# Four-layer graph network, one core: the third pass over the adjacency by half rows on four column groups

## The chip, the cores and the metric

The kernel runs on one core of one Trainium2 chip. The metric is the device time of one execution in microseconds (us), as a median of several runs. The engines are TensorE (PE), VectorE (DVE), ScalarE (ACT), GpSimd (POOL) and SyncE (SP), whose queue here issues most loads; ACT and POOL can issue DMAs too.

## The reference

`x` is 2708 x 128, `adj` a sparse 2708 x 2708 matrix with weights. Four layers follow each other, each as `x = layernorm(x + layer(x, adj))`:

```python
# layer 0: z = leaky(lap(A) x W1 + b1); S = exp(-dist(z) / 2), the 4 nearest of each row kept
out = _lap_mul(S + A, x) @ W2 + b2            # _lap_mul(A, x) = d * (A @ (d * x)), d = rowsum(A) ** -0.5
# layer 1
den = exp(leaky_relu(s_row[:, None] + s_col[None, :], 0.01))
num = A @ den
H   = A @ ((den / num) @ XW)                  # den / num where num != 0
# layer 2: h = (dinv * A * dinv) @ x; h @ W.T + b
# layer 3: relu([x, A @ x] @ W.T + b)
```

Layer 1 is the one that the change touches: `num` is a dense 2708 x 2708 product of `adj` with a matrix whose entries depend on a sum of a row number and a column number only.

## The kernel before, in words

**Tiling.** The rows of `adj` (its transpose `adjT` is streamed from HBM) are 22 row tiles: 21 full ones of 128 rows and a last one of 20 (`FULL = 21`). The 2708 columns are six chunks (four of 512, one of 384, one of 276), or two halves of 1354 (`HALF`). Row tiles 16 to 21 stay resident (`res`); tiles 0 to 15 (`S = 16`) are streamed again in each pass over `adj`.

**Order of the whole.** Pass one (degrees and A x, L428), the search for nearest neighbours (L699 to L702, bound by DVE), pass two (`by_panels`, L189, with a queue `due` of small steps that have due times), then the third pass (L1316 to L1396), then a block loop for layer 1 (`block_layer`, from L1556, 44 steps), then layers 2 and 3 with passes of their own.

**How layer 1 avoids the dense product.** Rows and columns are sorted by rank, and the sorted `num` is computed in 22 x 2 blocks (`NQ = 22` groups of columns, two halves). Within a block the change from one row to the next is a short list of rows of `adj`: `slot_i` lists them, POOL gathers them from HBM into `ring` (L1449, two gathers a step), `lw` holds their weights. A chain of four blocks (`CH = 4`, 11 chains, `NCH`) hands its last row on through `carry` (SP: L1586 writes, L1455 reads back). The chains' first rows come from the third pass.

**The third pass.** It computes 22 sums, `A` times a 128 x 22 weight matrix per row tile (`lc`, 32 columns wide, 22 used), and puts them into `carry`. By column chunk `c` the 20 row tiles 0 to 19 go in groups of four to the four groups of 32 columns of PE, so four different row tiles add up side by side in one bank (`part_sum`, matmul L1322). Tile 20 and the last 20 rows of three chunks go to these groups together. So at the end four partial sums per chunk have to be folded: `end_sums(c)` copies the bank on ACT (L1331), multiplies by the 0/1 matrix `sel` on PE (L1333) and copies into `carry` on ACT (L1334). It is called behind the first panel of chunk c + 1, for the last chunk behind everything. `fold` and `sel` are built in the neighbour search by six DVE operations.

A streamed panel is 4 row tiles by one chunk (1 MB, rows of 2,048 bytes). Six slots hold such panels: four in `ring` and two in `more`, all filled ahead of the pass (L178 is the load).

**Work in between.** `between(c, i0)` (L1338) puts the sorting work on PE, DVE and ACT between the panels, in an order written out by hand: `last_xw`, `find_blocks`, `into_places` (L1169, tiles `js` and `sl`), `count` (L1255, L1262), `ranked` (POOL: memset of `xws` L1193 and then `SOON` = 14 fetches of X W rows, L1039), `listed` (L1279, gives `slot_i`), and six groups of `weights` (transposes L1058 on PE, then ACT L1308 for groups 1 and 3, DVE L1312 to L1314 for the others).

**Into the block loop.** A flag read from the chip chooses the branch (L1464). Then ACT loads a table (L1561), the first num (L1571) waits for gathers, the rows out of `carry` and the weights; Ln (L1403), Exp (L1406), err (DVE L1413), L1417, L1420 follow, then hacc (PE L1428). Each of the first eight steps also carries one of the remaining fetches (L1039) on POOL.

Of the kernel before, what the change touches and what calls it, by code (L numbers as in the profile page):

```python
# [8 lines left out]
F32 = mybir.dt.float32  # L9
# [7 lines left out]
P = 128  # L17
CW = 512
# [3 lines left out]
KC = 126  # L22
CH = 4
MAGIC = 1.5 * 2**23
OOB = 4095
# [5 lines left out]
class Due:  # L31
# [5 lines left out]
    def at(self, n, f, *args):  # L37
        self.work.append((n, len(self.work), f, args))
        self.work.sort(key=lambda w: w[:2])
# [13 lines left out]
def kernel(  # L53
# [16 lines left out]
    nc = tc.nc  # L70
# [7 lines left out]
    C = len(starts)  # L78
# [17 lines left out]
    def few(c):  # L96
        g = c % GROUPS * 32
        return slice(g, g + LAST)
# [12 lines left out]
    def acc_tile():  # L111
        return acc_pool.tile([P, CW], F32, tag="acc", name="acc")

    def mis_tile():
        return mis_pool.tile([P, CW], F32, tag="mis", name="mis")
# [55 lines left out]
    def load_panel(g, c, pool=None):  # L171

        if pool is None:
            s = slots[taken[0] % len(slots)]
            taken[0] += 1
        else:
            s = pool.tile([P, 4, CW], F32, tag="strip", name="part")
        nc.sync.dma_start(  # L178
            s[:, :, : cw[c]],
            adjT[g * 4 * P : (g + 1) * 4 * P, cols[c]].rearrange("(t p) k -> p t k", p=P),  # L180
        )
        return s
# [587 lines left out]
    rows_h = atile([1], "rows_h")  # L770
    spare = near.rearrange("p t k -> p (t k)")
    few_n, rk_f, neg_r = (spare[:, n * T : (n + 1) * T] for n in range(3))
    fold, sel = spare[:, 3 * T : 3 * T + 2 * NCH], spare[:, 3 * T + 2 * NCH : 3 * T + 2 * NCH + 2 * NB]
    nc.vector.memset(rk_f, float(OOB))
    nc.vector.tensor_add(fold, ident[:, : 2 * NCH], ident[:, 32 : 32 + 2 * NCH])
    for g in (64, 96):
        nc.vector.tensor_add(fold, fold, ident[:, g : g + 2 * NCH])
    nc.vector.memset(sel, 0.0)
    nc.vector.tensor_copy(
        sel.rearrange("p (a v) -> p a v", v=2 * CH)[:, :, :2], fold.rearrange("p (a v) -> p a v", v=2)  # L780
    )
    nc.vector.memset(rows_d, 0.0)
    add_bias(b2_sb)
    rk = rk_pool.tile([P, T], F32, tag="rk", name="rk")
# [182 lines left out]
    near_at = [24 + (23 * t) // 5 for t in range(T)]  # L967
    for t in range(T):
        at(near_at[t], sum_near, t)

    ended = [-16]
    behind_last = []
# [48 lines left out]
        due.flush()  # L1021
    late.close()
    more = ExitStack()
    more_pool = more.enter_context(tc.tile_pool(name="more", bufs=2, side="right"))
    slots += [more_pool.tile([P, 4, CW], F32, tag="more", name="more") for _ in range(2)]
    taken[0] = 0
    G = S // 4
    panels = [(c, g) for c in range(C) for g in range(G)]
    ready = [load_panel(g, c) for c, g in panels[: len(slots)]]
    sums.close()  # L1030
    lwx = ctx.enter_context(tc.tile_pool(name="lwx", bufs=1))
    val_q = lwx.tile([P, T, 3, NQ], F32, tag="xws", name="val_q")
    val_b = lwx.tile([P, T, 3, NB], F32, tag="lw", name="val_b")
    plain = lwx.tile([P, 2], F32, tag="plain", name="plain")

    SOON = 14

    def fetch_xw(xws, q):
        nc.gpsimd.indirect_dma_start(  # L1039
# [5 lines left out]
    with tc.tile_pool(name="rank", bufs=1) as rank:  # L1045
# [38 lines left out]
        def to_all(c_part):  # L1084
            n = c_part.shape[-1]
            out = mis_tile()
            nc.tensor.matmul(out[:, :n], lhsT=ones_f, rhs=c_part, start=True, stop=True)
            return out
# [27 lines left out]
        def last_xw():  # L1116

            for t in last_ts:
                p = pw[t]
                pt = mis_tile()  # L1120
                nc.tensor.transpose(pt[:, :p], xs[:p, t, :], ident[:p, :p])
                xT = small.tile([P, P], F32, tag="z", name="xT")
                nc.scalar.copy(xT[:, :p], pt[:, :p])
                po = mis_tile()
                nc.tensor.matmul(po[:p, :D], lhsT=xT[:, :p], rhs=wa_sb, start=True, stop=True)
                row = small.tile([P, P], F32, tag="junk", name="row")
                nc.scalar.copy(row[:p], po[:p, :D])
                nc.gpsimd.dma_start(xw_rows[t * P : t * P + p, :], row[:p])
# [185 lines left out]
            nc.vector.tensor_scalar_max(w, w, 0.0)  # L1314

        carry = big.tile([P, NQ * P], F32, tag="y", name="carry")  # L1316
        sums_of, begun = {}, set()

        def part_sum(c, i, g, src, rows=slice(None), last=False):
            if c not in sums_of:  # L1320
                sums_of[c] = acc_tile()
            nc.tensor.matmul(  # L1322
                sums_of[c][32 * g : 32 * g + 32, : cw[c]], lhsT=lc[rows, i, :], rhs=src,
                start=(c, g) not in begun, stop=last,
            )
            begun.add((c, g))

        def end_sums(c):
            w = cw[c]
            tot = rank.tile([P, CW], F32, tag="tot", name="tot")  # L1330
            nc.scalar.copy(tot[:, :w], sums_of[c][:, :w])  # L1331
            ps = mis_tile()
            nc.tensor.matmul(ps[: 2 * NB, :w], lhsT=sel, rhs=tot[:, :w], start=True, stop=True)  # L1333
            nc.scalar.copy(carry[: 2 * NB, cols[c]], ps[: 2 * NB, :w])  # L1334

        work = {}

        def between(c, i0):  # L1338

            if (c, i0) == (0, 4):  # L1340
                last_xw()
            if (c, i0) == (0, 8):
                c_edge = to_all(c_part)
                find_blocks(c_edge)
                work["js"] = js_pool.tile([P, CW], F32, tag="places", name="js")
            if (c, i0) == (1, 4):
                for n in range(3):
                    into_places(work["js"], hot[n], val_q[:, :, :2, :], n)
                hot.append(ones_at(b_j, 3))
                find_values()  # L1350
            if (c, i0) == (2, 0):
                work["counts"] = count()
            if (c, i0) == (2, 4):
                into_places(work["js"], hot[3], val_q[:, :, :2, :], 3)
                find_places(*work["counts"])
                work["xws"] = ranked(work["js"])
                hot[:] = [ones_at(pos, n, spot) for n in range(3)]
            if (c, i0) == (3, 0):
                work["sl"] = js_pool.tile([P, CW], F32, tag="places", name="sl")
                for n in range(3):  # L1360
                    into_places(work["sl"], hot[n], val_b, n)
                hot.append(ones_at(pos, 3, spot))
            if (c, i0) == (3, 4):
                into_places(work["sl"], hot[3], val_b, 3)
                work["lw"] = listed(work["sl"])
            if (c, i0) in ((3, 8), (3, 12), (3, 16), (4, 0), (4, 4), (4, 8)):
                weights(work["lw"], 4 * work["groups"])
                work["groups"] += 1

        work["groups"] = 0  # L1370
        nc.vector.tensor_reduce(lone_part, lone, AX.X, ALU.add)
        for c in range(C):
            w = cw[c]
            begins = c % GROUPS == 0
            for i0 in range(0, FULL - 1, 4):
                if i0 < S:
                    n = c * G + i0 // 4
                    part = ready[n] if n < len(ready) else load_panel(i0 // 4, c)
                for i in range(i0, i0 + 4):
                    src = part[:, i % 4, :w] if i < S else res[:, i - S, cols[c]]  # L1380
                    part_sum(c, i, i % 4, src, last=i0 + 4 >= FULL - 1 and (i % 4 > 0 or not begins))
                if i0 == 0 and c:
                    end_sums(c - 1)
                if i0 + 4 >= FULL - 1 and begins:
                    for n in range(c, c + GROUPS):
                        part_sum(n, FULL - 1, n - c, res[:, FULL - 1 - S, cols[n]])
                    for n in range(c, c + GROUPS):
                        part_sum(n, FULL, 0, res[few(n), FULL - S, cols[n]], few(n), last=n == c)
                    if c == 0:
                        ps = mis_tile()  # L1390
                        nc.tensor.matmul(ps[:, :1], lhsT=ones_f, rhs=lone_part, start=True, stop=True)
                        nc.scalar.copy(lone_all, ps[:, :1])
                between(c, i0)
        xws, lw = work["xws"], work["lw"]
        end_sums(C - 1)
        order.close()  # L1396
    del slots[SLOTS:]
    more.close()

    def invert(w, num, pool, bufs, sums=True):  # L1400
# [44 lines left out]
    def load(i):  # L1445
        h, q = steps[i]
        rows[i] = strip(i).rearrange("p (n k) -> p n k", n=2)
        for n in range(2):
            nc.gpsimd.indirect_dma_start(  # L1449
                out=rows[i][:KC, n, :], out_offset=None, in_=adj_half[:, :],  # L1450
                in_offset=bass.IndirectOffsetOnAxis(ap=slot_i[h][:KC, 2 * q + n : 2 * q + n + 1], axis=0),
                bounds_check=2 * N - 1, oob_is_err=False,
            )
            b = block(2 * q + n)
            nc.sync.dma_start(  # L1455
                rows[i][KC : KC + 2, n, :], carry[2 * b : 2 * b + 2, h * HALF : (h + 1) * HALF]
            )

    m_rows = row_tile("m_rows").rearrange("p (t d) -> p t d", d=D)
    mT = m_rows.rearrange("p t d -> p (t d)")[:, :N]  # L1460
# [306 lines left out]
```

## Time and profile before

| | us |
|---|---|
| three runs | 1094.03, 1094.39, 1097.14 |
| median | 1094.39 |
| profiled execution | 1093.01 |
| its span | 1091.3 |
| PE busy (share of the span) | 1000.2 (92%) |
| DVE busy | 638.5 (59%) |
| ACT busy | 336.6 (31%) |
| POOL busy | 265.2 (24%) |
| mean granted PE clock | 0.965 |
| third pass, first add (L1322) | 459.82 |
| last add of the third pass | 524.48 |
| first num of the block loop (L1571) | 530.06 |
| first Ln (L1403) | 533.92 |

How to read it: a line of the timeline gives start, duration, engine, source line, operation, result `<-` operands with partitions x elements, how many records, and in brackets the idle time before it and what ended that. PE records of a float matmul are several to a matmul, so `x8` can be four matmuls; matmuls on different column groups of PE overlap. "SPq" is SP's queue, "remote" a releaser that the trace doesn't name.

### The profile page before, as it was taken

The numbers are of one execution on the slowest core, as the hardware profiler recorded it, in microseconds if no ns is written. First come the engines' busy times: TensorE is split into PE (matmuls) and PEld (weight loads), VectorE is DVE, ScalarE is ACT, GpSimd is POOL, SyncE is SP. The second block draws the span as 40 slices with busy tenths as digits, with TensorE's granted clock in tenths as the row PEclk, the third lists the DMA queues.
The fourth block names the chain that finished last, engine by engine and source line by source line (L and its number), as shares of the span: only waits on it lengthen the run. The fifth ranks groups of instructions, "written<-read, shape, count | busy, mean of one in ns | idle before, by whom it ended". The sixth has DMA issues, their size and how long they took to land.

```text
span 1091.3 us, 11487 instructions
## 1 busy us (share of the span) xinstructions
PE 1000.2 (92%) x3697; PEld 482.7 (44%) x3697; DVE 638.5 (59%) x1363; ACT 336.6 (31%) x617; POOL 265.2 (24%) x339
## 2 busy tenths in 40 slices
PE   0898999999987898798799999999999999999996
PEld 0445544444433455543233333334444644565444
DVE  5885448999934477772499999998112112132122
ACT  0000126555401144612467776665001100011000
POOL 4000000000575463015584344430112100000000
PEclk9889999999997899798899999999999999999998
DMA  9999340000383556497545545555775865574752
GB/s 341 357 329 276 102 137 1 0 1 1 100 279 89 186 160 205 141 369 228 136 131 153 154 122 166 143 143 181 230 232 157 275 229 183 170 238 158 240 158 77
DMA packets 109380, 190.31 MB, mean 174 GB/s; under 512 B 13666, under 2 KB 46706, under 8 KB 109310
## 3 DMA queue, kind: packets, MB, share of 16 engines
q1 hardware_dynamic: 91408, 151.79, 42.7%
q0 software_dynamic: 17728, 37.62, 12.5%
q8 instruction: 31, 0.51, 0.2%
q14 instruction: 39, 0.32, 0.1%
q10 hardware_dynamic: 174, 0.08, 0.0%
HBM read 214.37 MB, written 4.16 MB: 200 GB/s over the span
## 4 chain that ended last, share of the span: by engine, by line
PE 66%; DVE 16%; DMA 6%; issue 4%; ACT 3%; another core or an unknown queue 2%; POOL 2%; SPq 1%; POOLq 0%; DVEq 0%; ACTq 0%
PE acc L204 31%; PE num L1571 9%; PE hacc L1428 9%; PE acc L428 7%; DVE where L702 6%; DVE near L701 5%; DMA res<-in_adjT 3%; PE acc L1322 2%; PE mis L285 1%; PE acc L699 1%; DMA part<-in_adjT 1%; DMA got<-y_rows,where 1%; ACT junk L911 1%; DVE both L483 1%
## 5 line engine op out<-in xcount | busy, mean ns | idle before, releaser
L1449 POOL DMA_INDIRECT ring<-in_adjT,slot_i x88 | 95.4, 1084 | 117.7 <-PE num L1571 88.8
L1571 PE MATMUL num<-ring,lw 128*64 128x512 f32 (+1 forms) x528 | 115.6, 560 | 3.3 <-DVE err L1413 1.4
L1428 PE MATMUL hacc<-inv,xws 128*128 128x512 f32 (+1 forms) x264 | 111.7, 559 | 0.6 <-issue 0.3
L699 PE MATMUL acc<-zT,z 128*128 128x512 f32 (+2 forms) x252 | 102.2, 552 | 0.0
L1403 ACT ACTIVATE inv<-num,plain 128x1024 f32<-128x1024 f32 x88 | 80.6, 916 | 60.9 <-PE num L1571 38.6
L253 POOL TENSOR_TENSOR rstd<-rstd,minus_half 128x4 f32<-128x4 f32 (+1 forms) x18 | 17.3, 961 | 313.4 <-DVE rstd L252 313.4
L234 ACT COPY gb<-acc 128x512 f32<-128x512 f32 (+2 forms) x18 | 9.6, 535 | 251.1 <-PE acc L204 251.1
L1413 DVE TENSOR_TENSOR err<-inv,num 128x1024 f32<-128x1024 f32 x88 | 74.4, 854 | 20.4 <-ACT inv L1406 17.6
L700 ACT COPY key<-acc 128x512 f32<-128x512 f32 (+2 forms) x126 | 67.1, 535 | 55.1 <-issue 27.9
L204 PE MATMUL acc<-ring,y 128*128 128x512 f32 (+2 forms) x192 | 81.8, 556 | 0.5 <-issue 0.5
L1428 PEld LDWEIGHTS hacc<-inv,xws 128*128 128x128 f32 x264 | 46.5, 189 | 77.6 <-issue 45.2
L729 POOL DMA_INDIRECT got<-y_rows,where x66 | 70.2, 1063 | 37.5 <-DVE near_sum L742 18.9
L204 PE MATMUL acc<-ring,xs 128*128 128x512 f32 (+2 forms) x192 | 77.9, 549 | 0.0
L1420 DVE SCALAR_TENSOR_TENSOR inv<-gb,g_inv,inv 128x1024 f32<-128x1024 f32 x88 | 77.0, 913 | 0.1
L204 PE MATMUL acc<-ring,carry 128*128 128x512 f32 (+2 forms) x192 | 74.5, 542 | 0.0
L204 PE MATMUL acc<-ring,m_rows 128*128 128x512 f32 (+2 forms) x192 | 74.3, 542 | 0.0
L1417 DVE SCALAR_TENSOR_TENSOR inv<-err,inv 128x1024 f32<-128x1024 f32 x88 | 72.4, 861 | 0.1
L1406 ACT ACTIVATE inv<-inv 128x1024 f32<-128x1024 f32 x88 | 67.6, 768 | 2.8
L699 PEld LDWEIGHTS acc<-zT,z 128*128 128x128 f32 x252 | 45.8, 190 | 50.4 <-issue 45.0
L575 POOL TENSOR_TENSOR slot_e<-near,sim 128x44 f32<-128x44 f32 (+2 forms) x3 | 0.7, 245 | 269.7 <-DVE d2inv L603 267.6
L1571 PEld LDWEIGHTS num<-ring,lw 128*64 128x64 f32 x528 | 36.2, 138 | 65.0 <-issue 46.7
L701 DVE MAX8 near<-key 128x8 f32<-128x2708 f32 x21 | 62.2, 2964 | 2.7 <-ACT key L700 2.7
(378 smaller groups left out, 1392.0 us busy)
## 6 DMA issues: line engine op xcount, KB each, us to landing
ring<-in_adjT SPq DMA_DIRECT2D x86, 1024.0 KB
ring<-in_adjT SPq DMA_DIRECT2D x19, 768.0 KB
part<-in_adjT SPq DMA_DIRECT2D x12, 1024.0 KB
ring<-in_adjT SPq DMA_DIRECT2D x19, 552.0 KB
res<-in_adjT SPq DMA_DIRECT2D x4, 1280.0 KB
more<-in_adjT SPq DMA_DIRECT2D x4, 1024.0 KB
part<-in_adjT SPq DMA_DIRECT2D x3, 768.0 KB
part<-in_adjT SPq DMA_DIRECT2D x3, 552.0 KB
```

The source lines that it names most:

```text
L204: nc.tensor.matmul(accs[c][: lhsT.shape[-1], :w], lhsT=lhsT, rhs=src, start=start, stop=stop)
L428: nc.tensor.matmul(accs[c][:, : cw[c]], lhsT=y[:, i, :], rhs=src[:, : cw[c]], start=first, stop=last)
L699: nc.tensor.matmul(pks[c][:p, : cw[c]], lhsT=z2[:, :p], rhs=zT[:, cs], start=False, stop=True)
L701: nc.vector.max(near[:p, t, :], key[:p])
L729: nc.gpsimd.indirect_dma_start(out=got[:p, :], out_offset=None, in_=y2_rows[:, :], in_offset=bass.IndirectOffsetOnAxis(ap=where[:p, t, k : ...
L1403: nc.scalar.activation(inv, num[:, :w], AF.Ln, scale=plain[:, 0:1], bias=plain[:, 1:2])
L1413: nc.vector.tensor_mul(err, inv, num[:, :w])
L1417: nc.vector.scalar_tensor_tensor(inv, err, 2.0, inv, op0=ALU.subtract, op1=ALU.mult)
L1420: nc.vector.scalar_tensor_tensor(inv, gb[:, col : col + w], g_inv[:, q : q + 1], inv, op0=ALU.max, op1=ALU.mult)
L1428: nc.tensor.matmul(haccs[:, o:e], lhsT=xws[:, q, :], rhs=inv[:, o:e], start=(q == 0), stop=(q == NQ - 1))
L1449: nc.gpsimd.indirect_dma_start(out=rows[i][:KC, n, :], out_offset=None, in_=adj_half[:, :], in_offset=bass.IndirectOffsetOnAxis(ap=slot_i[ ...
L1571: nc.tensor.matmul(num[n * (BJ + 2) : (n + 1) * (BJ + 2), o:e], lhsT=lw[:, 2 * q + n, :], rhs=rows[i][:, n, c0 + o : c0 + e], start=True, ...
```

## The change

- The third pass goes by *lines*: one row tile by half of the columns (128 x 1354, 693 KB, rows of 5,416 bytes). The four column groups of PE take four quarters (339, 339, 338, 338 columns) of one row tile, all with the same weights, so the bank holds finished sums and nothing is folded. Order: first half, then second half, 16 lines each.
- Nine *berths* hold lines: six half strips of `ring` and three in `more`, filled ahead of the pass. Load n + 9 is issued behind line n. Lines from 27 on use only the three in `more`.
- The resident tiles' halves (`own_line`) and the last 20 rows (`add_last_rows`) stand between the lines. For the latter the last rows are loaded again by quarters into other partition groups (8 small SP loads), and put back after the pass (6).
- At the end of each half two ACT copies take the bank to `heads`, and four DMAs on ACT's queue put its rows into `carry`, partitions 96 to 117; `load` takes a chain's first rows from there.
- The order by hand is the list `turns`. `fold`, `sel` and their six DVE operations go; the memset of `rk_f` moves into pass two.
- `SOON` is 6: six fetches of X W rows ahead of the loop, sixteen in its steps.

The core of the diff:

```diff
-    for g in (64, 96):
-        nc.vector.tensor_add(fold, fold, ident[:, g : g + 2 * NCH])
...
+    at(20, nc.vector.memset, rk_f, float(OOB))
...
+    berths = [ring[:, n * HALF : (n + 1) * HALF] for n in range(2 * STRIPS)]
+    berths += [more_pool.tile([P, HALF], F32, tag="more", name="more") for _ in range(3)]
+    AHEAD = len(berths)
+    lines = [(i, h) for h in range(2) for i in range(S)]
+    def line_at(n):
+        return berths[n % AHEAD if n < 3 * AHEAD else AHEAD - 3 + n % 3]
+    def load_line(n):
+        i, h = lines[n]
+        nc.sync.dma_start(line_at(n), adjT[i * P : (i + 1) * P, h * HALF : (h + 1) * HALF])
...
-    SOON = 14
+    SOON = 6
...
-            nc.scalar.copy(tot[:, :w], sums_of[c][:, :w])
-            ps = mis_tile()
-            nc.tensor.matmul(ps[: 2 * NB, :w], lhsT=sel, rhs=tot[:, :w], start=True, stop=True)
-            nc.scalar.copy(carry[: 2 * NB, cols[c]], ps[: 2 * NB, :w])
...
+        for g in range(4):
+            for h in range(2):
+                n0, n1 = h * HALF + edges[g], h * HALF + edges[g + 1]
+                nc.sync.dma_start(res[few(g), FULL - S, n0:n1], adjT[FULL * P :, n0:n1])
+        def add_line(i, h, src, last=False):
+            for g in range(4):
+                nc.tensor.matmul(
+                    banks[h][32 * g : 32 * g + 32, : edges[g + 1] - edges[g]], lhsT=lc[:, i, :],
+                    rhs=src[:, edges[g] : edges[g + 1]], start=(h, g) not in begun, stop=last,
+                )
+                begun.add((h, g))
+        def add_last_rows(h):
+            for g in range(4):
+                n0, n1 = h * HALF + edges[g], h * HALF + edges[g + 1]
+                nc.tensor.matmul(
+                    banks[h][32 * g : 32 * g + 32, : n1 - n0], lhsT=lc[few(g), FULL, :],
+                    rhs=res[few(g), FULL - S, n0:n1], start=False, stop=False,
+                )
+        def end_half(h):
+            tot = heads[:, h * span : (h + 1) * span]
+            nc.scalar.copy(tot[:, : edges[4] - edges[3]], banks[h][:, : edges[4] - edges[3]])
+            nc.scalar.copy(tot[:64, edges[4] - edges[3] :], banks[h][:64, edges[4] - edges[3] : span])
+            for g in range(4):
+                w = edges[g + 1] - edges[g]
+                nc.scalar.dma_start(
+                    carry[HEADS : HEADS + 2 * NCH, h * HALF + edges[g] : h * HALF + edges[g + 1]],
+                    tot[32 * g : 32 * g + 2 * NCH, :w],
+                )
...
+        def line(n):
+            for _ in range(n):
+                at = loaded[0]
+                loaded[0] += 1
+                i, h = lines[at]
+                add_line(i, h, line_at(at), last=at == 2 * S - 1)
+                if at + AHEAD < 2 * S:
+                    load_line(at + AHEAD)
...
+        turns = [
+            (line, 4), (blocks_of_edges,), (line, 5), (own_line, 2), (last_xw,), (in_rank_order, 0), (line, 2),
+            (in_rank_order, 1), (line, 2), (in_rank_order, 2), (count_lone,), (line, 2), (counts,), (line, 1),
+            (add_last_rows, 0), (own_line, 3), (line, 2), (ranks_known,), (line, 2), (own_line, 1), (in_list_order, 0),
+            (line, 2), (in_list_order, 1), (in_list_order, 2), (line, 2), (own_line, 1), (in_list_order, 3), (line, 1),
+            (next_weights,), (next_weights,), (line, 1), (own_line, 1), (next_weights,), (line, 2), (next_weights,),
+            (own_line, 1), (line, 1), (next_weights,), (line, 1), (next_weights,), (own_line, 1), (add_last_rows, 1),
+            (line, 2),
+        ]
...
+            nc.sync.dma_start(res[few(c), FULL - S, cols[c]], adjT[FULL * P :, cols[c]])
+        end_half(1)
...
-                rows[i][KC : KC + 2, n, :], carry[2 * b : 2 * b + 2, h * HALF : (h + 1) * HALF]
+            at = 2 * b if b % CH else HEADS + b // CH * 2
+            nc.sync.dma_start(rows[i][KC : KC + 2, n, :], carry[at : at + 2, h * HALF : (h + 1) * HALF])
```

## The prediction

> **What bounds the kernel now.** I read the shares by engine first (TensorE, PE, is busy for 92% of the span at a mean clock of 0.965), then a table of ten-microsecond windows around the third pass (460 to 530 us), then PE's timeline there, then those of GpSimd (POOL), the load queue (SPq) and ScalarE (ACT). The windows (columns: PE, PEld, DVE, ACT, POOL busy with counts; granted clock; DMA share; GB/s):
>
> ```profile
> 450.00:460.00 10.00, 7.76 (x89) 6.84 (x93) 8.78 (x28) 6.93 (x14) 0.28 (x1) 0.52 0.01 2
> ...
> 470.00:480.00 10.00, 10.00 (x83) 5.64 (x84) 8.80 (x20) 1.23 (x3) 0.00 (x0) 1.00 0.99 360
> 480.00:490.00 10.00, 10.00 (x87) 4.45 (x83) 4.31 (x11) 1.50 (x4) 2.40 (x1) 1.00 1.00 359
> 490.00:500.00 10.00, 10.00 (x82) 6.36 (x74) 3.48 (x9) 1.17 (x2) 7.77 (x8) 1.00 1.05 362
> 500.00:510.00 10.00, 7.47 (x45) 2.11 (x44) 1.79 (x3) 2.09 (x8) 7.04 (x7) 1.00 0.71 215
> 510.00:520.00 10.00, 8.42 (x52) 3.24 (x52) 4.58 (x9) 4.00 (x12) 1.33 (x2) 0.66 0.43 117
> 520.00:530.00 10.00, 4.39 (x44) 1.54 (x36) 0.43 (x1) 1.73 (x4) 6.06 (x6) 0.89 0.63 166
> ```
>
> From 470 to 500 us PE and the DMA engines are both full. From 500 on both have holes: the streaming is nearly done, and the tail of short serial steps decides. PE's own lines there:
>
> ```profile
> 508.60 0.48 PE L1322 MATMUL acc<-more,lc 128*32 128x384 f32 x1 [0.21 <-issue]
> 511.58 2.01 PE L1333 MATMUL mis<-tot,near 128*88 128x512 f32 x2 [2.50 <-ACT tot L1331]
> ...
> 522.25 0.88 PE L1333 MATMUL mis<-tot,near 128*88 128x384 f32 x2 [1.96 <-issue]
> 523.06 0.67 PE L1322 MATMUL acc<-ring,lc 128*32 128x276 f32 x8
> 523.55 1.11 PE L1322 MATMUL acc<-more,lc 128*32 128x276 f32 x16
> 524.48 0.65 PE L1322 MATMUL acc<-res,lc 128*32 128x276 f32 x8
> 528.31 1.22 PE L1333 MATMUL mis<-tot,near 128*88 128x276 f32 x2 [3.19 <-ACT tot L1331]
> 530.06 6.51 PE L1571 MATMUL num<-ring,lw 128*64 128x512 f32 x20 [0.52 <-ACT carry L1334]
> ```
>
> The fold (L1333) stands on PE's own path, and the last one delays num of the first block. The other engines wait behind the same tail:
>
> ```profile
> 508.05 1.00 POOL L1039 DMA_INDIRECT xws<-xw_rows,row_j  x1 [0.30 <-issue]
> 518.36 1.07 POOL L1449 DMA_INDIRECT ring<-in_adjT,slot_i  x1 [9.31 <-PE acc L1322]
> ```
> ```profile
> 533.92 1.20 ACT L1403 ACTIVATE inv<-num,plain 128x1024 f32<-128x1024 f32 x1 [2.43 <-PE num L1571]
> ```
>
> 533.92 is where the block loop really begins: ACT's Ln, then err, keep and the next rows follow it at fixed distances, and 44 steps of about 4.9 us (PE: 2.43 num + 2.47 hacc). I reckon the change as a shift of this one time.
>
> **The change, part by part.**
>
> Bytes: unchanged, 22.18 MB through the load queue. Before the pass 6 panels (6.29 MB) lie ready, then 9 lines (9 x 0.693 = 6.24 MB); either way the queue rests in 450 to 460 (2 GB/s) and 15.9 MB (23 lines) are left from 461 us.
>
> PE's adds: eight 512-wide records (four matmuls beside each other on the four column groups) add 0.86 us, eight 276-wide 0.46, so about 1.67 ns a column; a line (339 columns) takes 0.57. With 42 of them, 24 us, and 1.1 for the last rows, the adds stay at about 25 us (before 26). Nothing there.
>
> Removed: six folds of about 1.0 us, twelve ACT copies (0.39 to 0.59) and PE's three stalls for tot, 2.50 + 1.96 + 3.19 = 7.65. Those after 505 (three folds and the stalls, 11 us) stand in the tail; the earlier three are PE time that covers DMA, worth nothing while both are full. The removed DVE operations for sel take about 1.0 us in the kNN stage, some 0.3 on the chain: gain 0.3. The memset moved to step 20 of pass two lies beneath PE: 0 (0.2 if uncovered).
>
> Line rate: a packet of 2,048 bytes takes 84 ns in the trace and one of 5,416 bytes 208; on 16 engines 390 and 416 GB/s. The windows reached 360, so by the same ratio I take 382 GB/s: 1.82 us a line. A rule speaks against this: the Trainium skill, "DMA: Bandwidth & Descriptors", section "Where 436 GB/s comes from", puts the limit of one core's HBM share at about 358 GB/s for loads into SBUF, whatever the row. By it a line takes 1.94 us. The windows at 359 to 362 agree with it, the 2.25 us slices of 440 to 530 (the transfer view's row of GB/s) do not:
>
> ```profile
> GB/s 257 308 360 340 0 0 0 0 7 33 325 402 385 378 398 383 388 206 340 353 397 395 385 373 367 368 335 231 233 56 271 38 236 15 191 142 130 121 174 244
> ```
>
> From the twelfth on (465 us) most stand at 373 to 402; I take 1.82, which lies below these peaks since dips come between; the rule makes everything below 2.6 us later.
>
> Where the stream ends: the order of the built program has a point that the words of the change don't tell. Loads 27 to 31 go to berths 6, 7, 8, 6, 7 and are issued right behind lines 18 to 22, while lines 24 to 26 still have to be read from these berths. So SP waits only for the earlier load into the same berth, and PE at line 24 waits for load 30, at 25 for 31, at 26 for 29. (Lines 24 to 31 so read the rows of tiles 14, 15 and 13 of half 1.) Behind line 24 on PE are queued six groups of weight transposes, seven lines, three own lines and the last rows, and behind those the weights' products on ACT and DVE. Landing of load 30: 461 + 1.5 latency + 22 x 1.82 = 502.5; plus the six early X W fetches, 0.4 MB = 1.05; plus the first six gathers (1.62 MB), whose strips come free with line 23, so that they run at about 496 to 505 instead of 518 to 527 and share the engines: half of their 4.2 us, and their issue among lines, 3.5. T30 = 507.
>
> PE gets to line 24 at about 495 (its timeline before reaches the end of the listing, L1169 sl, at 498.4 with three folds more and part of the adds shifted), so it idles 12 us. Idle PE is granted half clock afterwards (0.52 in 450:460; periods of 6.83 us at 0.5): a line then costs 1.13 and a group of four transposes 1.06, not 0.57 and 0.65.
>
> Tail behind T30: 11 lines x 0.57 = 6.3; the groups, the last a half one, 3.7; the last rows 0.6; and in a period of 6.83 us at half clock work of 3.8 us gets done: 3.0 more. Sum 13.6 to PE's end, 12.5 to the last rows, as two lines stand behind them. One rule weighs on the last rows: the Trainium skill, "TensorEngine Tiling (Array Packing)", "Gotcha 1: PSUM Pressure": different row tiles cannot use one PSUM bank at once. The change puts all four into one bank, before they went to three banks (about 1.0 us for six records). By the rule they take 4 x 0.57 = 2.3 instead of 0.6: 1.7 us more. I take 0.6, since row groups 0, 32, 64 on separate columns stand nearest that row, and keep 1.7 for the range.
>
> From there two ways lead to the first Ln. SP: the last of six copies that restore the last rows (0.37) waits for the last rows on PE; then the branch's flag (0.51), a row from carry (0.61) and its landing (2.0): num(0) at T30 + 16.0. ACT, from PE's end: two copies (0.65), four row DMAs (about 0.48 each), then their landing, or the flag (0.6) and the table (1.28) beside it (2.2): Ln at T30 + 18.4 = 525.4, which is also num(0) and 2.4, a whole num at full clock (before 3.9, at 0.77). Before: 533.92. Gain 8.5.
>
> SP's fourteen extra small DMAs ahead of pass three, issue 0.37 each, 5 us, stand behind panel waits that are longer (SPq waits 48.9 us for L1322 alone): 0; uncovered they would cost at most 5.
>
> Six X W rows, not fourteen: eight fetches of 1.31 = 10.5 us leave POOL's queue ahead of the gathers. POOL was behind PE there anyway (9.31 idle), so 0 by itself. In the loop steps 0 to 15 now carry a fetch, before 0 to 7: 2 x 1.35 + 1.31 = 4.0 us a step, under 4.9. I take 0; bounds 0 and 3 us, since POOL's 4.03 us at L253 already cost PE some 2 us at 566.8 and recovers slower with fetches behind it.
>
> Sum: 1093.0 (the profiled execution; its span 1091.3 and 1.7 around it) - 8.5 - 0.3 = 1084.2. The median shown is 1.4 above the profiled run: 1085.5.
>
> **Rivals.**
> - Stream at the packets' rate: lines of 1.67 us (416 GB/s) and gathers that take nothing from them: T30 = 461 + 1.5 + 36.7 + 1.05 = 500.2, Ln at 518.6, gain 15.3: about 1079. For it: slices at 400 GB/s; against: no ten-microsecond window above 362. It cannot be better by much, as PE itself is at 495.
> - The wait at line 24 eats everything: 1.94 us a line (T30 = 509.6), 1.7 for the last rows, and a late signal from PE. The trace has PE's signals to ACT and SP delayed: ACT's weights waited to 507.91 and tot to 510.94, 4 to 9 us after the matmuls, in a stretch of back-to-back POOL fetches. With 4 us of that Ln stands at 533.8: 1094.
> - Slower: POOL becomes the bound of the loop in steps 8 to 15. Each carries a fetch more; if a gather beside it took not 1.35 but 2.5 us, the step would be 6.3, and PE would lose 1.4 x 8 = 11.2, with the 3 us at L253 more than the 8.8 won: 1085.5 + 14.2 = about 1100. It costs from a POOL step of 4.9 us on and turns the sign from 5.6 ((8.8 - 3) / 8 = 0.7). For it: the first eight steps of before, which carry a fetch, ran in 4.3 to 4.9 on POOL, so there is little room; against it: POOL's gathers waited 88.8 us for num in all, so PE led.
> - That nothing is gained because the folds weren't in the way is excluded by L1333's 3.19 ahead of num.
>
> **How the numbers follow.** Chances: forecast case (gain 4 to 13) 0.62, packet rate 0.14, eaten up 0.15, POOL 0.09. About 0.3% (3.3 us) is what a measurement of this kernel can tell from no change. Faster 0.78 (the first two and a part of the third), same 0.12, slower 0.10. Range 1078 to 1095: from the packet rate to just past the eaten gain.
>
> **What would show it.** No L1333; PE idle of 8 to 15 us ahead of a line, released by a DMA, about 495 to 507; clock 0.5 behind it; the first gathers at 496; Ln at 525; the distance Ln to end unchanged (557 us). The prediction is wrong if PE doesn't stop at line 24, if the rows of heads or SP's restoring come later than num's other inputs by over 3 us, or if the steps 8 to 15 run longer than 4.9.

## The result and the profile after

| | before | changed |
|---|---|---|
| median of four runs, us | 1094.74 | 1087.42 |
| profiled execution, its span | 1093.01, 1091.3 | 1089.06, 1087.3 |
| pass three: first add to last add | 65.3 | 63.2 |
| pass three: first add to first Ln | 74.1 | 69.6 |
| first Ln to last Ln of the block loop | 215.7 | 216.5 |
| first Ln to the end of the span | 557.4 | 559.7 |

The ratio of the times is 0.9946, with a 95% interval of 0.9921 to 0.9972. The prediction was 1085.5. In the traces the time from the first add of pass three to the first Ln is the best measure, since the starts of the pass lie between 456 and 461 us in the runs on chips like this one, and what stands ahead of it moves the whole. I call that time *the stretch*, and give times inside it from its start where I compare kernels. The stretch fell by 4.5 us, where the prediction had 8.5. The gain of 7.3 us between the medians is more than the profiled executions show (4.0), and its interval goes from 3 to 9 us.

One thing has to be known with all these numbers. As the prediction says in brackets, the loads 27 to 31 overwrite three berths that lines 24 to 26 have yet to read. So lines 24 to 31 multiply the rows of tiles 13, 14 and 15 with the weights of tiles 8 to 15: for the second half of the columns the changed kernel leaves out the rows of tiles 8 to 12. This is an error of the change, and the times here are those of a kernel with it. Run 1 below gives each line its own rows, and its time is the same within the noise.

The same ten-microsecond windows after the change (columns as in the prediction):

```profile
450.00:460.00 10.00, 8.72 (x76) 6.66 (x80) 8.75 (x26) 5.65 (x15) 0.28 (x1) 0.54 0.01 2
...
470.00:480.00 10.00, 10.00 (x86) 5.62 (x86) 6.80 (x16) 0.16 (x1) 0.00 (x0) 0.85 1.02 413
480.00:490.00 10.00, 10.00 (x118) 5.34 (x117) 5.93 (x12) 0.82 (x4) 2.59 (x2) 1.00 0.77 289
490.00:500.00 10.00, 8.14 (x76) 5.29 (x75) 1.66 (x7) 0.00 (x0) 6.03 (x6) 1.00 0.97 369
500.00:510.00 10.00, 2.58 (x14) 1.50 (x15) 0.23 (x2) 0.00 (x0) 7.34 (x7) 0.51 1.04 310
510.00:520.00 10.00, 8.83 (x94) 3.56 (x96) 5.81 (x11) 4.93 (x16) 0.00 (x0) 0.98 0.33 81
```

Two things to see: from 470 to 480 the stream runs at 413 GB/s where before it ran at 360, and the hole of PE has moved to 500 to 510, where the DMA engines are full. It is the wait for load 30, in PE's timeline:

```profile
507.42 1.35 PE L1330 MATMUL acc<-more,lc 128*32 128x339 f32 x8 [8.49 <-DMA more<-in_adjT]
...
511.81 0.78 PE L1330 MATMUL acc<-more,lc 128*32 128x339 f32 x8 [1.17 <-DMA more<-in_adjT]
...
519.85 1.34 PE L1330 MATMUL acc<-more,lc 128*32 128x339 f32 x16
522.68 4.91 PE L1609 MATMUL num<-ring,lw 128*64 128x512 f32 x20 [1.49 <-DMA ring<-carry]
```

The tail behind it, from 507.42 to PE's end at 521.19, is serial. POOL no longer waits for it: it issues six fetches, then the gathers from 500.06. On ACT the four row DMAs of the second half stand right ahead of the table load and Ln:

```profile
521.78 3.27 ACTq L1354 DMA_DIRECT2D carry<-heads  x4
526.06 1.28 ACT L1599 ACT_TABLE_LOAD   x1 [4.31 <-SPq L1801]
527.61 1.21 ACT L1442 ACTIVATE inv<-num,plain 128x1024 f32<-128x1024 f32 x1 [0.26 <-PE num L1609]
```

And there is a hole of the stream at 486 to 490, which the prediction did not have. It stands in the load queue's own list of waits (us in total, times, longest):

```profile
SPq L1028 <- DMA more<-in_adjT: 11.0, 5, 2.8
SPq L1028 <- DMA carry<-heads: 6.4, 1, 6.4
```

The second line is the hole: load 24 waited for the row DMAs of the first half, which touch none of its memory. The built program, as I read it, has one of its eight completion counters used by both, so that the later user waits for the earlier one; the trace shows the wait, not the counter. Runs 2 and 5 test it. The first line I read as the waits of loads 27 to 31, which SP issued from 492.72 to 502.54, for earlier loads into the same three berths.

### The profile page after: what moved, and what is told of

Same layout as the page of the kernel before. It is cut to its first block, busy times and chain, and to the rows that moved or that the text cites. A ratio compares the mean times of both kernels' runs of the same rounds, so it can differ in the third digit from the quotient of the medians.

```text
span 1087.3 us, 11655 instructions
## 1 busy us (share of the span) xinstructions
PE 993.7 (91%) x3773; PEld 484.8 (45%) x3773; DVE 637.1 (59%) x1358; ACT 331.4 (30%) x609; POOL 271.8 (25%) x339
## 3 DMA queue, kind: packets, MB, share of 16 engines
q0 software_dynamic: 17728, 37.62, 12.6%
## 4 chain that ended last, share of the span: by engine, by line
PE 49%; DVE 1%; ACT 1%; issue 1%; DMA 0%; POOL 0%; POOLq 0%; DVEq 0%
PE acc L204 27%; PE num L1609 10%; PE hacc L1467 9%; PE mis L285 1%; PE mis L1740 0%; DVE inv L1456 0%; DVE err L1452 0%; ACT gb L234 0%; PE mis L1706 0%; DVE inv L1459 0%; PE mis L1736 0%; DMA ring<-carry 0%; ACT inv L1442 0%; POOL rstd L253 0%; ACT inv L1445 0%
## 5 line engine op out<-in xcount | busy, mean ns | idle before, releaser
L1488 POOL DMA_INDIRECT ring<-in_adjT,slot_i x88 | 101.0, 1148 | 105.9 <-PE num L1609 81.9
L729 POOL DMA_INDIRECT got<-y_rows,where x66 | 69.9, 1059 | 36.9 <-DVE near_sum L742 17.0
L699 PEld LDWEIGHTS acc<-zT,z 128*128 128x128 f32 x252 | 45.8, 190 | 50.4 <-issue 45.0
L1609 PEld LDWEIGHTS num<-ring,lw 128*64 128x64 f32 x528 | 36.1, 138 | 66.6 <-issue 47.2
```

The costliest lines, as they stand in the source:

```text
L699: nc.tensor.matmul(pks[c][:p, : cw[c]], lhsT=z2[:, :p], rhs=zT[:, cs], start=False, stop=True)
L729: nc.gpsimd.indirect_dma_start(out=got[:p, :], out_offset=None, in_=y2_rows[:, :], in_offset=bass.IndirectOffsetOnAxis(ap=where[:p, t, k : ...
L1488: nc.gpsimd.indirect_dma_start(out=rows[i][:KC, n, :], out_offset=None, in_=adj_half[:, :], in_offset=bass.IndirectOffsetOnAxis(ap=slot_i[ ...
L1609: nc.tensor.matmul(num[n * (BJ + 2) : (n + 1) * (BJ + 2), o:e], lhsT=lw[:, 2 * q + n, :], rhs=rows[i][:, n, c0 + o : c0 + e], start=True, ...
```

## The experiments

Twelve runs, on four chips. On two of them the kernel before takes 1090 to 1093 us, on two about 1061; the text says which it was. A ratio compares with the kernel before on the same chip. Times within the stretch come from one trace each. "The changed kernel" means the trace of the result above, on a chip where before takes 1094 ("the first chip"), unless run 10 is named: on the chip of runs 1 to 4 it was not run itself. In runs 1 and 8 each line has its own rows; runs 2 to 7, 10 and 12 have the error of the changed kernel.

### 1 to 4: on the chip with before at 1093 (42 runs)

**Own berths** (e1).

```diff
-        return berths[n % AHEAD if n < 3 * AHEAD else AHEAD - 3 + n % 3]
+        return berths[n % AHEAD if n < 3 * AHEAD else n - 3 * AHEAD + 4]
...
-                if at + AHEAD < 2 * S:
+                if at + AHEAD < 3 * AHEAD:
                     load_line(at + AHEAD)
+                elif 3 * AHEAD - 5 <= at < 2 * S - 5:
+                    load_line(at + 5)
```

> Edit: loads 27 to 31 go to berths 4 to 8, each issued behind the line that read the berth (22 to 26), so that line 24 no longer waits for load 30. Theory (the wait of line 24 and the serial work behind it set the end): PE doesn't stop for 8.5 us at line 24; it waits in pieces at the last lines, the weights' transposes run in between; PE's last add moves from 521.2 to about 511 to 513, the first Ln from 527.6 to about 519, and the time falls by 7 to 8 us, to about 1080. Rival (the end of the stream sets it, whatever PE does before): PE's last add moves by less than 3 us and the time by less than 2.

Measured: 1085.56, ratio 0.9947 (0.9921 to 0.9973), as the changed kernel's own. PE does not stop at line 24 any more and the transposes run in between, but loads 27 to 31 now wait for PE, run beside the gathers and end late: PE's last line comes at 520.3, the last add 60.4 after the start (63.2), the first Ln 68.1 (69.6). The stretch won 1.5 us, not 7. So the end of the stream counts too, and not only the work behind line 24, as the theory had it. How much each counts this trace can't say, since it also carries 3.2 us of half clock more than the changed kernel's (see run 6). The time didn't move.

**First half's row DMAs later** (e2): `end_half(0)` moved behind `in_list_order(3)` in the list.

> Edit: the copies and four row DMAs of the first half (end_half(0)) are issued behind the last listing step, not behind the last own line of half 0. Theory (load 24 waited 6.4 us for these DMAs to land, since it shares a completion counter with them): the hole in the stream at 484 to 489 us goes, load 30 lands at about 501 instead of 507.1, and the time falls by about 5.5 us, to about 1082. Rival (PE's own work held the stream there, all berths being full): load 30 lands at most 2 us earlier, the time falls by less than 2.

Measured: 1089.33, ratio 0.9973 (0.9951 to 0.9995); load 30 at 48.9 after the start, not 49.4. This edit did not do what it was for: between the two places ACT has hardly any work, so ACT issued them only some 3 us later (491.03), and then load 25 waited for them, to 493.32. The wait went with the DMAs from load 24 to load 25, as a shared counter would have it, but the edit decides nothing on the cost; the fifth run is the proper one.

**SOON = 14** (e3).

> Edit: SOON = 14 again, the rest as in the changed kernel. Theory (POOL is off the path ahead of the loop and under 4.9 us a step in it): first gathers at 510 instead of 500, still ahead of the first num; the time within 1.5 us of the changed kernel's. Rival one (late fetches cost in the loop, which was 0.8 us longer from first to last Ln): 1 to 3 us faster. Rival two (the earlier gathers are what won): 2 us or more slower; but the gathers then don't take from the lines, so load 30 may land up to 3 us earlier.

Measured: 1090.28, ratio 0.9978 (0.996 to 0.9995). The stretch is 70.2 us, the landing of load 30 48.2 (49.4): the gathers took 1.2 us from the lines, not the 3.5 of the prediction. The loop from first to last Ln took 214.8 (216.5). The time lies between the theory and the second rival: the changed kernel's ratio of 0.9946 would be 1087.2 on this chip, and the two intervals overlap. The trace also shows what made me look again: DVE's first step behind the listing, which PE had ended at 499.5, began at 511.85, when POOL's fourteen fetches were over.

**Weights first** (e4): in `turns`, own lines, the six groups and the last rows of half 1 ahead of line 24, then `(line, 8)`.

> Edit: only the order by hand: the own lines, the six groups of weights and the last rows of half 1 stand ahead of line 24, lines 24 to 31 behind everything. Line 24 still waits for load 30. Theory (the work queued behind line 24 is what costs): PE's idle time is filled, behind load 30 only eight lines of 0.6 us are left instead of 13.8 us of work, PE's last add at about 513 to 514, Ln at about 520, the time falls by about 7, to about 1080. Rival (what counts is the landing of the loads and the chain over ACT's row DMAs behind it): the last add moves, but Ln by less than 3 us.

Measured: 1084.07, ratio 0.992 (0.9888 to 0.9951). Last add 59.1 (63.2), Ln 65.3 (69.6): 4.3 us of the 7 expected. Load 30 lands as before (49.9), but line 25 then waits for load 31, to 53.2; in the changed kernel that wait is mostly filled with transposes. The work behind line 24 does cost, at least 4 us of the 13.8: this trace too carries 3.2 us of half clock more (see run 6), so the saving may be larger. By the times alone it is not shown, since the interval overlaps that of the changed kernel.

### 5 to 8: on a chip with before at 1061 (29 runs)

**First half's rows on POOL's queue** (e5): `nc.scalar.dma_start` becomes `(nc.scalar if h else nc.gpsimd).dma_start`.

> Edit: the four row DMAs of the first half go on POOL's queue, not ACT's, so that no load of the stream shares a completion counter with them (the edit before had only moved them by one load: load 25 then waited for them, to 493.3). In the changed kernel load 24 was issued 30.7 us after the pass began and load 30 landed at 49.4. Theory (these DMAs hold the stream): load 24 is issued at about 25, the hole of 3 us goes, load 30 lands at about 46, the first Ln comes 3 us earlier after the pass's start (66.5, not 69.6), and the time falls by 3 us against the changed kernel's. Rival (all nine berths were full and PE held the stream anyway): load 30 lands less than 1 us earlier, no change.

Measured: 1067.39, ratio 1.0069 (1.0041 to 1.0097), against 1.0107 of the changed kernel (run 10, on a chip of the same kind). Load 24 is issued 24.4 us after the start (30.8 in run 10), load 30 lands at 45.4 (49.6 in run 10), Ln comes at 64.6 (69.9). Without a counter shared with the stream 4 to 5 us are gone: the theory holds, with more than its 3. But before was faster than all of these, which nothing in my account explained.

**Second half's rows late** (e6): the four DMAs go into a list, out of `m_rows`' memory, and steps 16 to 19 of the loop issue one each on POOL.

> Edit: the row DMAs of the second half are issued in steps 16 to 19 of the block loop, from POOL, out of a buffer of their own (their rows are needed from step 20 on); the first half's stay on ACT. Theory (ACT issued them for 3.3 us ahead of its table load and the first Ln): Ln follows num(0) by about 2.4 to 3 us, not by 4.9, at 67.2 after the pass's start, not 69.6; the time falls by about 2.4. Rival (the flag or the table load was late in any case, or the loop loses it again): Ln moves by less than 1 us.

Measured: 1073.09, ratio 1.0103 (1.0073 to 1.0132). Its ACT:

```profile
512.41 1.28 ACT L1609 ACT_TABLE_LOAD   x1 [0.15 <-issue]
515.91 1.20 ACT L1452 ACTIVATE inv<-num,plain 128x1024 f32<-128x1024 f32 x1 [2.22 <-PE num L1619]
```

And that of run 10, where num(0) began at 506.49 and Ln waited for the row DMAs:

```profile
512.23 1.20 ACT L1442 ACTIVATE inv<-num,plain 128x1024 f32<-128x1024 f32 x1 [1.07 <-DMA carry<-heads]
```

In run 6 num(0) began at 513.18, so Ln stands 2.7 us behind it, as expected, and 5.7 us in run 10. But the time did not fall (1071.52 in run 10), and the stretch is 72.5 us, not 69.9: load 30 landed at 52.2 instead of 49.6. In this execution ACT waited 11.65 us for a product of PE (L1373; L1363 in the changed kernel, where it waited 8.45): 3.2 us are lost ahead. The same wait of 11.65 or 11.66 stands in the traces of runs 1, 4 and 12. PE's mean clocks in three-microsecond windows (9 to 21 us after the start: 0.66, 0.50, 0.50, 0.63 in run 4, much the same in runs 1, 6 and 12) make about 10.2 us at half clock there, in the changed kernel (0.91, 0.52, then 1.00) about 3.4; the 6.8 us between them cost half. So the saving behind num is shown, and in this execution probably eaten by the clock ahead of it; the traces of one run each can't say more, and why the median of six didn't fall stays open.

**All of it, weights first** (e7): the edits of 4, 5 and 6 together.

> Edit: both of these, and the order with weights, own lines and last rows ahead of line 24. If the three savings are separate they add up: the last add at about 56 after the pass's start (59.1 with the order alone, 63.2 in the changed kernel), Ln at about 60 (65.3, 69.6), the time 9 to 10 us under the changed kernel's, about 1078. If they overlap (each hides what the next would show), Ln stays above 63.

Measured: 1060.41, ratio 0.9999 (0.998 to 1.0019). Last add 54.8, Ln 57.6: the three savings add up (69.9 to 57.6), and the result is just before's time.

**All of it, own berths** (e8): the edits of 1, 5 and 6.

> Edit: both of these, and loads 27 to 31 in berths 4 to 8, each behind the line that frees its berth, so that no line waits for a later one's load. With the berths alone the stream ended 6 us later, since these loads then waited for PE and ran beside the gathers: last add 60.4 after the pass's start, Ln 68.1. Expected with the others: last add at about 57, Ln at about 62, the time about 7 under the changed kernel's. If gathers and lines only share one full set of DMA engines, the last add stays at about 60 and Ln comes at 64.

Measured: 1065.09, ratio 1.0045 (1.0028 to 1.0063); last add 55.0, Ln 63.1. Num(0) began at 500.44, 3.8 us after the last add, when its row had landed. Worse than 7; it is also the only one of the combined versions in which every line has its own rows.

### 9 and 10: both kernels, unchanged, on one chip with before at 1061

> The kernel before, unchanged, once more with a trace of its own, beside the changed kernel on one chip. The second set of experiments ran on another chip, where the kernel before took 1061 us (1093 on the first), pass two 130 us, not 147, and where PE's signals to DVE and ACT came at once; on the first they came up to 11 us late while POOL issued fetches back to back. Theory (late PE signals made the tail of before's third pass long, and the change won by moving fetches out of it): where signals come at once, before goes from the pass's start to the first Ln in about 60 to 64 us; where they come late, in about 74 (as in the first profile). Rival (the chips differ only elsewhere): 74 in both.

> The changed kernel, unchanged, on the same chip as the run above. Theory: its own stretch from the pass's start to the first Ln is set by load 30 and the work behind it, so it stays at 66 to 70 us on either chip; on a chip with prompt signals the changed kernel is then slower than before by 4 to 8 us (ratio about 1.006), on one with late signals faster by 5 to 7 (about 0.994). Rival: it gains 5 to 7 us on both.

Measured: before 1060.07 (ratio 0.9997, 0.9976 to 1.0017), changed 1071.52, ratio 1.0107 (1.0075 to 1.0139). **On this chip the change is slower by 1.1%.** The stretch of the changed kernel is 69.9 us here and 69.6 on the first chip; that of the kernel before is 58.6 here and 74.1 there. The tail of before on this chip (PE, then ACT):

```profile
488.88 1.09 PE L1333 MATMUL mis<-tot,near 128*88 128x512 f32 x2
...
495.00 0.88 PE L1333 MATMUL mis<-tot,near 128*88 128x384 f32 x2 [0.19 <-issue]
...
498.44 0.70 PE L1333 MATMUL mis<-tot,near 128*88 128x276 f32 x2 [0.56 <-ACT tot L1331]
499.66 4.31 PE L1571 MATMUL num<-ring,lw 128*64 128x512 f32 x20 [0.52 <-ACT carry L1334]
```
```profile
484.82 2.46 ACT L1308 ACTIVATE lw<-mis,slot_f,slot_e 128x62 f32<-128x62 f32 x8 [8.91 <-PE mis L1058]
```

The same folds that waited 2.50, 1.96 and 3.19 us wait 0, 0.19 and 0.56. And ACT's first group of weights, which PE's transposes of 484.13 release, starts at 484.82. On the first chip those transposes stand at 500.97, and ACT started here:

```profile
500.97 0.65 PE L1058 MATMUL mis<-ident,g_col 128*128 128x128 f32 x4
507.91 2.46 ACT L1308 ACTIVATE lw<-mis,slot_f,slot_e 128x62 f32<-128x62 f32 x8 [15.15 <-remote]
```

That is six us after they had ended, near the end of POOL's fourteen fetches (490.33 to 509.05). On this chip the same fetches ran too (473.49 to 492.23), and nothing waited for their end. Even on the first chip not every signal was late during them: DVE took up PE's listing, ended at 498.47, without delay, and only the next product, ended at 500.05, 2.1 us late:

```profile
498.55 0.31 DVE L1285 TENSOR_SCALAR slot_i<-sl 128x44 uint32<-128x44 f32 x2 [4.79 <-PE sl L1169]
...
502.17 0.68 DVE L1312 TENSOR_TENSOR lw<-mis,slot_e 128x496 f32<-128x496 f32 x1 [2.29 <-PE mis L1058]
```

Another place shows it with the same kernel: in pass two, DVE's L785 follows PE's L780 and POOL issues fetches back to back. The changed kernel on the first chip, then on this one:

```profile
339.84 1.12 DVE L785 SCALAR_TENSOR_TENSOR xs<-mis,d2inv,xs 128x128 f32<-128x128 f32 x4 [10.86 <-remote]
```
```profile
331.55 1.13 DVE L785 SCALAR_TENSOR_TENSOR xs<-mis,d2inv,xs 128x128 f32<-128x128 f32 x4 [2.16 <-PE mis L780]
```

PE's L780 began at 330.11 there and at 329.75 here. All traces agree at this place (L794 where the kernel is the one before): DVE begins 2.6 to 8.7 us after PE's product has ended in the eight traces of chips where before takes 1090 or more, and 0.05 us or less after it in the six of chips where before takes 1061. I call the first kind *late signals* and the second *prompt*; whether the signal of PE is late or the engine that waits for it, the traces don't say.

### 11 and 12: on a second chip with late signals (before at 1090, 27 runs)

**Before with SOON = 6** (e11), one number of the kernel before.

> One part of the change alone: the kernel before with SOON = 6, the third pass by panels and with folds as it was. On a chip whose PE signals come late while POOL issues fetches back to back (before at about 1093): theory, the run of fourteen fetches in the tail made them late, so with six the stretch from the pass's start to the first Ln falls from 74 to about 60 to 63 and the time by 10 to 13 us, more than the whole change won; rival, the folds and their waits made the tail, then no change. On a chip with prompt signals (before at about 1061): within 1.5 us of before by both, 58.6 us for the stretch, unless the eight fetches more in the loop cost something (1 to 3 us slower).

Measured: 1085.43, ratio 0.9957 (0.9936 to 0.9978); the stretch is 67.8 us. One number gives nearly what the whole change gave on the first chip (0.9946). It stops short of the 60 to 63 expected, since POOL's gathers and a fetch (seven in a row, 507.42 to 516.98) now hold up the last sum in the same way; ACT's lines show the first group in time and the last copy not:

```profile
499.37 2.46 ACT L1308 ACTIVATE lw<-mis,slot_f,slot_e 128x62 f32<-128x62 f32 x8 [8.91 <-PE mis L1058]
...
517.81 0.39 ACT L1331 COPY tot<-acc 128x276 f32<-128x276 f32 x1 [6.88 <-remote]
```

PE's last add had ended at 512.42. From first to last Ln the loop took 214.1 us, not longer than before's 215.7: the late fetches cost nothing there (in run 3 fourteen early ones went with a loop shorter by 1.7 us than the changed kernel's, so the two runs disagree in sign).

**The combined version again** (e12, the kernel of 7).

> The version by half rows with weights first, the first half's row DMAs on POOL and the second half's late, once more. It took the stretch from the pass's start to the first Ln in 57.6 us where before took 58.6. On a chip with late signals (before 1093, stretch 74): if its short runs of fetches keep clear of them, 58 to 60 us again, the time 14 to 16 us under before's, about 1078; if not, over 65. On a chip with prompt signals: within 2 us of before, as measured.

Measured: 1076.99, ratio 0.9885 (0.985 to 0.9919); the stretch 59.8 us. PE and ACT of this run:

```profile
516.13 4.31 PE L1618 MATMUL num<-ring,lw 128*64 128x512 f32 x20 [0.63 <-ACT m_rows L1354]
```
```profile
518.25 1.20 ACT L1451 ACTIVATE inv<-num,plain 128x1024 f32<-128x1024 f32 x1 [0.80 <-PE num L1618]
```

It is faster than before on a chip with late signals, and level with before where signals are prompt (run 7). The changed kernel did not run on this chip; its interval on the first, 0.9921 to 0.9972, lies just above. Both runs still have the error in lines 24 to 31, and the combined version without it, run 8, was not run on a chip with late signals.

## Why the prediction was right, and where it wasn't

The sign and the size on the first chip were right, 7.3 us in the medians against 8.9 predicted, but in good part by luck. The traces have only 4.5 us in the stretch instead of 8.5; the pass began 1.8 us earlier, and behind the first Ln 2.3 were lost that should have been 0. The mechanism of the changed kernel's own stretch, a wait for load 30 and a serial tail, was foreseen. What the change took *away from before* was not: the step that failed is the removed part, "three folds and the stalls, 11 us".

Put side by side, the stretches on chips with late signals (one trace each, on three chips) show what gained:

| | fourteen early fetches | six early fetches |
|---|---|---|
| third pass as before | 74.1 | 67.8 (run 11) |
| third pass by half rows | 70.2 (run 3) | 69.6 |

With fourteen fetches the pass by half rows is shorter by 3.9 us, with six it is longer by 1.8, and with prompt signals the changed kernel's is longer than before's by 11.3 (58.6 and 69.9). So the new pass gained only where it took the place of a tail that late signals had made long.

- **Folds and their waits.** They are gone, but most of their price was not theirs. Where signals are prompt the stalls are 0.75 us in all (run 9), not 7.65. On the first chip I read "2.50 <-ACT tot" as a cost of the fold; ACT itself had started late behind PE. The rival that the folds weren't in the way, which the prediction excluded by the 3.19 ahead of num, was nearer to it: that wait is 0.56 in run 9.
- **"Six X W rows, not fourteen: 0 by itself."** Failed. Run 11 shows this one number worth 6.3 us of the stretch (74.1 to 67.8, on two chips of the same kind) and 4.7 us in the time, by ratio nearly as much as the whole change. I had the evidence in hand: the rival with "a late signal from PE" names the fetches, but puts the lateness on the changed kernel, where PE waits for a DMA while they run, and not on before, where it was in the trace.
- **The wait at line 24.** Right: PE stood 8.49 us for load 30. I had it landing 47.2 us after the start (507 in before's time); it was 49.4. Two terms were off and nearly cancelled. The line rate: 410 to 419 GB/s over three-microsecond windows from 464 to 482 us, 1.67 us a line where I took 1.82, so 22 x 0.15 = 3.3 us earlier. The hole from the shared completion counter: 4.2 us later (run 5 against run 10), a term I did not have. The gathers' share was 1.2, not 3.5. By these the landing would be at 45.8; the 3.6 us left are not assigned. PE was later along the lines than I had it (line 24 at 40.9 after the start, not 35), and loads wait for lines too. And loads 27 to 31 waited 11.0 us in all for earlier loads into their three berths, a wait that the prediction named and put at nothing: load 30 was issued only at 499.08. No run measures either by itself.
- **The limit of 358 GB/s**, which the prediction took from the Trainium skill, "DMA: Bandwidth & Descriptors", section "Where 436 GB/s comes from", as what binds loads from HBM, does not bind this stream: a ten-microsecond window at 413 stands above. The same passage also gives 425 GB/s as measured for a 16 MB load, which fits better.
- **The tail.** 13.8 us from line 24 to PE's end, 13.6 predicted, in part by luck. The clock was 0.51 in the window ahead of it, as predicted, but half clock ended at 510.44, 3.0 us into the tail, and so cost 1.5 us, not 3.0; and PE waited 1.17 us for load 31, which the sum did not have. The four last-row matmuls in one bank took 0.77 us for eight records, a line 0.75 to 0.78: nothing is added by sharing a bank here. So the 1.7 us that the prediction kept for the rule of the Trainium skill ("TensorEngine Tiling (Array Packing)", "Gotcha 1: PSUM Pressure") did not come.
- **num(0) and Ln.** 15.3 and 20.2 us behind load 30, predicted 16.0 and 18.4. ACT's row DMAs took 0.82 each, not 0.48. Run 6 shows the price of their place: without them 2.7 us from num to Ln instead of 5.7 in run 10 (4.9 on the first chip).
- **The loop.** 0.8 us longer from first to last Ln, inside the 0 to 3 bounded, and of the steps 8 to 15 only the first took longer than 4.9 (6.6); run 11 shows no cost of the sixteen late fetches by themselves. Behind the loop another 1.5 us were lost, which no run explains.
- **Slower.** My rival on the slow side (POOL in the loop) did not happen. Another did, on other chips: with the signals prompt, before needs 58.6 us and the changed kernel 69.9. The first half's row DMAs, with the counter, are 5.3 us of it (run 5), ACT's row DMAs some 3.0 (run 6), the order around line 24 4.3 (run 4, on a chip with late signals): 12.6 together, and run 7, with all three gone, took off 12.3 and ended level with before. That the sum agrees so well may be chance, as half clock may hide up to 3.2 us in run 4.

Open: what makes the signals late on the first chip and two of the four others. The traces show only when: during runs of seven or more fetches or gathers that POOL issues back to back, and up to about 3 us beyond, and not for every signal in them. That fewer fetches shorten the tail is shown by run 11, that their issue itself delays the signals is argued from it. That it is the chip, and not another condition that differed between the runs, is not tested either.

## What to carry to other kernels

A wait whose end the profile gives as "remote", or an engine that starts long after the one it waits for has ended, need not be a cost of the step it stands at: look for what else ran then, and change that alone first. Before a gain of half a per cent is believed, both kernels should run on more than one chip; here the sign differs. A DMA on another queue can hold up a stream without touching its data: look for it in the load queue's own list of waits, and try it on another queue, as run 5 did. And when buffers are filled ahead, check for each load that everything that still has to be read from its place stands before it; here five loads came too early.

## What the hardware showed that I had not expected

- Chips differ by 33 us on one kernel (1094 and 1061), 17 of them ahead of the third pass, where the same late signals stand in pass two, and 15.5 in the stretch (profiled executions on the first chip and in run 9).
- Loads of 5,416-byte rows on one core ran at 401 to 424 GB/s, in three-microsecond windows of the full stream, in the traces of the result and of runs 1, 3 to 6, 10 and 12.
- PE's half clock behind the gaps of `last_xw` lasts 3.4 or 10.2 us from execution to execution, worth 3.2 us, and of one and the same kernel in runs 7 and 12 (ACT's wait there 8.45 and 11.66 us); it may be part of the scatter of a kernel's runs (1087 to 1098 for before on one chip).
